# A later turn for attention's products, more steps in the gated layer, and other places for first-used tiles

## The chip, the cores and the metric

The kernel runs on one core of a Trainium2 chip. The metric is the device time of one launch in microseconds. Engines are named as in the profile: PE (matrix products), PEld (its weight loads), DVE, ACT, POOL (GpSimd) and SP, which here issues transfers. A line number such as L1310 is a line of the kernel before, also in the listing below.

## What is computed

Four residual blocks follow each other, each wrapped as x + layernorm(f(layernorm(x))): attention, a mixture of eight experts, attention with a distance bias, and a two-layer stack of local attention and gated feed-forward. x is 2 x 1024 x 128, f32. The change bears on the last block, and on its preparation, which runs during the third. One layer of the last block, cut to what matters:

```python
h = shift_token(x)                       # second half of the features from the token before
q, k, v = split(h @ wqkv, 3)             # 8 heads of 64
q = l2norm(q) * qs; k = l2norm(k) * ksc
q, k = rotary_xpos(q, k)
o = local_attention(q, k, v)             # windows of 64 that see themselves and the window before
x = x + o @ wo
h = layernorm(shift_token(x)) * lg + lb
a, g = split(h @ w1 + b1, 2)
x = x + (a * gelu(g)) @ w2 + b2
```

The stack has two such layers (l = 0, 1). Products are made to f32 accuracy: many are three products of high and low 16-bit parts (`mm3`, lines L49, L50, L51).

## The kernel before

The kernel has four phases. Phases 1 to 3 are the first three blocks. During phase 3, phase 4's preparation (constants, tables, normalization of the first half of x by L92, and the transposes of that into a product's layout by L231) is a generator, which is advanced by one `yield` at a time between pieces of phase 3's work.

Phase 4, the last stage, goes over 32 tiles of 128 tokens: layer l = i // 16, batch b = i // 8 % 2, tile t = i % 8. Each tile passes through small stages: `a` (q and k products and the first rotation products), `a1` and `a2` (norms and rotation), `b0` and `cast` (scaling, high 16-bit parts), `b1` (low parts L1236 and L1237, and three DMA transposes through SP that give K, Q and Qz), `v` (V projection, copied by ACT at L1256, and a shifted copy Vs by DMA), `kc`, `c` (score maxima: products L1277 and L1282, reduction into mz L1291), `c2` (transposes mz, L1296, and ACT copies it to mT, L1298), `d` (transposed scores, with the maxima subtracted by a product with mT at L1310; exponential p at L1316), `e` (attention times V L1327, reciprocal L1336, scaled u L1337), `e1` (transpose of the result L1344, copy oT L1346), and `f` (product with wo L1355, added to F at L1356).

A list, `plan`, names the stages with a lateness. In iteration i it calls each stage in list order for tile i minus its lateness, so up to six tiles are in work. The instructions of all calls are chained in that order on each engine (`in_order`): the plan sets the order of every queue, DMA queues included, and no scheduler moves anything across it.

The gated layer (`stage_g`) handles a group of tiles at once: four, and two for each of the last two groups. ENDS lists the tiles that close a group. It is a generator: at each `gated` entry of the plan, every open group is advanced to its next `yield`. Its steps: token shift by products with `sh` (SH: L1368 to L1371) into hc by POOL (L1372) and ACT (L1373); statistics (DVE L81 to L84, POOL L88); the factor nb (L97) and the normalization on ACT (L99); transposes of hc (L1384), gh and hg on ACT (L1388, L1389), their difference gl on DVE (L1391); nine products and gelu (L1398, each set between two loads of ACT's function table); nine more products; the gating (L1409); the product py (L1413) and yT on ACT (L1415); transposes (L1420) and the addition to F (L1422). In layer 1 the final normalization (L92), the residual (L1429) and the output transfer follow.

`aside` holds slower side work: `normalize(1)`, the second half's normalization, from iteration 1, and layer 1's weights from iteration 6. PSUM banks come in rings, with one name for the products of most stages (b).

K, V and Vs are rings of 5, 6 and 6 buffers. They are allocated in ascending order in memory that phase 3 partly still holds; V's extra column of constants is filled by six memsets at L1156, at the stage's start.

Of the kernel before, what the change touches and what calls it, by code (L numbers as in the profile page):

```python
# [10 lines left out]
F32 = mybir.dt.float32  # L11
F32R = mybir.dt.float32r
F16 = mybir.dt.float16
BF16 = mybir.dt.bfloat16
I32 = mybir.dt.int32
AF = mybir.ActivationFunctionType
ALU = mybir.AluOpType
# [226 lines left out]
def phase1(k, X):  # L244
# [9 lines left out]
    with ExitStack() as es:  # L254
# [61 lines left out]
        def values_of(pair, c):  # L316

            b, a = pair // 4, pair % 4
            xTh, xTl = S["x", b]
            vh, vl = V[pair % 2]  # L320
            ps = big().rearrange("p a (t n) -> p (a t) n", t=2)
# [684 lines left out]
def phase4(k, X):  # L1006
# [5 lines left out]
    nc, A = k.nc, k.A  # L1012
    H, HD, HID = 8, 64, 341
    WS = 256.0
    with ExitStack() as es:
# [7 lines left out]
        nc.gpsimd.dma_start(mask0, A["c_mask0"])  # L1023
        identb = cp.tile([128, 128], BF16, name="identb")
        nc.gpsimd.tensor_copy(identb, k.ident)

        pick = cp.tile([128, H, 128], F16, name="pick")
        nc.gpsimd.tensor_copy(pick, k.ident16[:, :H].unsqueeze(2).to_broadcast([128, H, 128]))
# [1 line left out]
        away = cp.tile([128, 128], F16, name="away")  # L1030
        nc.gpsimd.dma_start(away, A["c_away"])
        nc.gpsimd.tensor_tensor(pick, pick, away.unsqueeze(1).to_broadcast([128, H, 128]), ALU.add)
        fac = cp.tile([128, NT], F32, name="fac")
        nc.sync.dma_start(fac, A["c_fac"])

        sh = cp.tile([128, 2, 128], F32, name="sh")
        nc.sync.dma_start(sh, A["c_shift"])
        Z = [cp.tile([128, 4, 256], F16, name=f"Z{i}") for i in range(2)]
# [2 lines left out]
        for m in mTs:  # L1041
            nc.gpsimd.dma_start(m, A["c_rows4"][int(m is mTs[2])])
        for i in range(2):
            nc.gpsimd.memset(Z[i], 0.0)
            nc.gpsimd.memset(mz[i], 0.0)
        F = [cp.tile([128, NT, D], F32, name="F0")]

        def normalize(b):
            x = [X[:, NT * b + t, :] for t in range(NT)]
            dst = [F[b][:, t, :] for t in range(NT)]  # L1050
            if b:
                yield from k.ln_steps(cp, dst, lambda t: x[t])
                return
            mv, rstd = k.ln_stats(cp, lambda t: x[t])
            yield
            k.ln_to(cp, dst, lambda t: x[t], mv, rstd)
# [54 lines left out]
        def stage_x(l, b, c):  # L1111

            hTh = cp.tile([128, 512], F16, name="hTh", bufs=2)
            hTl = cp.tile([128, 512], F16, name="hTl", bufs=2)
            ps = k.transposed(ps_sm, F[b], c)
            k.split_r(hTh[0:64, :], hTl[0:64, :], ps[0:64, :])
# [21 lines left out]
        wp = pool("p4w", 1)  # L1138
        F.append(wp.tile([128, NT, D], F32, name="F1"))
        sp = pool("p4s", 2)  # L1140
# [3 lines left out]
        def bank(kind=None):  # L1144
            turn[0] = (turn[0] + 1) % 7
            return ps[turn[0] // 3].tile([128, 512], F32, name="b1")

        QB = 3
        RV = 6
        RK = 5  # L1150
        K = [wp.tile([128, H, 192], F16, name=f"K{i}") for i in range(RK)]
        V = [wp.tile([128, H, HD + 1], F32, name=f"V{i}") for i in range(RV)]
        Vs = [wp.tile([128, H, HD + 1], F32, name=f"Vs{i}") for i in range(RV)]
        xm = [wp.tile([128, 64], F32, name=f"xm{b}") for b in range(B)]
        for i in range(RV):
            nc.gpsimd.memset(V[i][:, :, HD : HD + 1], WS)  # L1156

        heads = lambda ap: ap.rearrange("p (h d) -> p h d", d=HD)
        where = lambda i: (i // 16, i // 8 % 2, i % 8)
# [68 lines left out]
        def stage_b1(i):  # L1228
# [5 lines left out]
            if t == 0:  # L1234
                nc.gpsimd.memset(K[k0][:, :, 0:64], 0.0)
            nc.gpsimd.tensor_tensor(mid4(k16), pair4(kk), ends(k16), ALU.subtract)  # L1236
# [4 lines left out]
            nc.sync.dma_start_transpose(Qz, fl(Z[i % 2]))  # L1241
            nc.sync.dma_start_transpose(K[k0][:, :, 64:192], fl(k16))
            nc.sync.dma_start_transpose(Q, fl(q16))
            S["q", i] = Q, Qz

        def stage_v(i):
            l, b, t = where(i)
            wvh, wvl = W[l][8:10]
            hTh, hTl = S["h", l, b, t // 4]
            ts = slice(128 * (t % 4), 128 * (t % 4) + 128)  # L1250
            v0, v1 = i % RV, (i + 1) % RV
            if t == 0:
                nc.gpsimd.memset(Vs[v0][0:64, :, :], 0.0)
            pv = bank("b")
            k.mm3(pv, hTh[:, ts], hTl[:, ts], wvh, wvl)
            nc.scalar.copy(V[v0][:, :, 0:HD], heads(pv))  # L1256
            nc.sync.dma_start(Vs[v0][64:128, :, :], V[v0][0:64, :, :])
            if t < NT - 1:
                nc.sync.dma_start(Vs[v1][0:64, :, :], V[v0][64:128, :, :])

        def stage_kc(i):

            t = where(i)[2]
            if t < NT - 1:
                dst = K[(i + 1) % RK][:, :, 0:64]
                nc.scalar.activation(dst, K[i % RK][:, :, 128:192], AF.Copy, scale=fac[:, t : t + 1])

# [33 lines left out]
        def stage_d(i):  # L1301
            l, b, t = where(i)
            k0 = i % RK
            mT, (Q, Qz) = S.pop(("m", i)), S.pop(("q", i))
            p = sp.tile([128, H, 2, 64], F32, name="p")
            for g in range(2):
                st = bank("d").rearrange("p (h w n) -> p h w n", h=4, w=2)
                for j in range(4):
                    h = 4 * g + j
                    nc.tensor.matmul(st[:, j, :, :], pick[:, 4 * (h % 2) + h // 2, :], mT, start=True, stop=False)  # L1310
                    for w in range(2):
                        kw = K[k0][:, h, 64 * w : 64 * w + 128]
                        s = slice(64 * w, 64 * w + 64)
                        nc.tensor.matmul(st[:, j, w, :], kw, Q[:, h, s], start=False, stop=False)
                        nc.tensor.matmul(st[:, j, w, :], kw, Qz[:, h, s], start=False, stop=w == 1)
                nc.scalar.activation(p[:, 4 * g : 4 * g + 4], st, AF.Exp)  # L1316
            S["p", i] = p
# [31 lines left out]
        def stage_f(i):  # L1349
# [4 lines left out]
            for a in range(4):  # L1354
                nc.tensor.matmul(ps, oT[:, a, :], wo[:, a, :], start=a == 0, stop=a == 3)  # L1355
            nc.vector.tensor_tensor(F[b][:, t, :], ps, F[b][:, t, :], ALU.add)  # L1356

        def stage_g(l, b, t0, T):

            w1h, w1l, w2, col = W[l][3:7]  # L1360
            x = F[b]
            g = slice(t0, t0 + T)
            n = 128 * T
            tiles = lambda ap: ap[:, :n].rearrange("p (t d) -> p t d", d=D)
            hc = tiles(sp.tile([128, 512], F32, name="hc"))
# [10 lines left out]
            yield  # L1376
            mv, rstd = k.ln_stats(sp, lambda t: hc[:, t, :], T)
            yield
            k.ln_scalar(sp, [hc[:, t, :] for t in range(T)], mv, rstd)
            yield  # L1380
            yield
            ps = bank()
            for t in range(T):
                nc.tensor.transpose(ps[:, 128 * t : 128 * t + 128], hc[:, t, :], k.ident)  # L1384
            hg = sp.tile([128, 512], F32, name="hg")[:, :n]
            gh = sp.tile([128, 512], F16, name="gh")[:, :n]
            gl = sp.tile([128, 512], F16, name="gl")[:, :n]
            nc.scalar.activation(gh, ps[:, :n], AF.Identity, scale=col[:, 7:8], bias=col[:, 8:9])  # L1388
            nc.scalar.activation(hg, ps[:, :n], AF.Identity, scale=col[:, 7:8], bias=col[:, 8:9])  # L1389
            yield  # L1390
            nc.vector.tensor_tensor(gl, hg, gh, ALU.subtract)  # L1391
            yield
            ges = []
            for i in range(3):
                pg = bank("g")[:, :n]
# [15 lines left out]
            py = bank()[:, :n]  # L1411
            for i in range(3):
                nc.tensor.matmul(py, w2[:, i, :], ges[i], start=i == 0, stop=i == 2)  # L1413
            yT = sp.tile([128, 512], F32, name="yT")[:, :n]
            nc.scalar.activation(yT, py, AF.Identity, bias=col[:, 6:7], scale=1 / WS)  # L1415
            yield
            yield
            ps = tiles(bank())
            for i in range(T):
# [3 lines left out]
            if l == 1:  # L1423
                mv, rstd = k.ln_stats(sp, lambda t: x[:, t0 + t, :], T)
# [8 lines left out]
        ENDS = [3, 7, 11, 15, 19, 23, 27, 29, 31]  # L1433
        gated, aside = [], []

        def advance(gens):
            gens[:] = [g for g in gens if k.in_order(next, g, 0) is None]


        plan = [  # L1440
            (stage_b0, 1), (stage_v, 2), (stage_a, 0), (stage_c2, 3), (gated, 0), (stage_d, 3), (stage_e1, 4),
            (stage_a1, 0), (stage_cast, 1), (stage_f, 5), (gated, 0), (stage_x, 0), (stage_c, 2), (stage_b1, 1),
            (stage_kc, 2), (aside, 0), (gated, 0), (stage_a2, 0), (gated, 0), (stage_e, 3), (aside, 0),
        ]
        i = 0
        while i < 32 + 5 or gated:
            if i == 1:
                aside.append(normalize(1))
                own = es.enter_context(k.pool("p4v", 1, "right"))
                late_weights = weights(1, own, lambda shape: own.tile(shape, F32, name=f"w{shape[1]}"))  # L1450
                k.in_order(next, late_weights)
            if i == 6:
                aside.append(late_weights)
            for f, late in plan:
                n = i - late
                if isinstance(f, list):
                    advance(f)
                elif f is stage_x:
                    if i - 5 in ENDS:
                        l, b, t = where(i - 5)  # L1460
                        T = i - 5 - ([-1] + ENDS)[ENDS.index(i - 5)]
                        gated.append(stage_g(l, b, t - T + 1, T))
                    if i % 4 == 3 and i + 1 < 32:
                        l, b, t = where(i + 1)
                        k.in_order(stage_x, l, b, t // 4)
                elif 0 <= n < 32:
                    k.in_order(f, n)
            i += 1


# [178 lines left out]
```

## Time and profile before

| | us |
|---|---|
| median of 3 runs | 1412.56 (1412.06 to 1414.65) |
| the profiled execution | 1407.81 |
| its span | 1406.0 |
| mT copies (L1298) in iterations 8, 24, 28, 32 (tiles 5, 21, 25, 29) start at | 1082.9, 1262.3, 1305.4, 1351.6 |

| engine | busy us | share of the span |
|---|---|---|
| PE | 1166.7 | 83% |
| DVE | 1050.4 | 75% |
| ACT | 968.2 | 69% |
| POOL | 879.4 | 63% |

The page divides the span into 40 slices of 35.15 us and gives busy tenths:

```profile
PE   4889999999889787757998986688657988988786
DVE  6776666776672798979888789873577778878875
ACT  2877777887665584532898785578567777787674
POOL 1666766786656545642776659575688776757541
```

The last stage begins at about slice 29 and holds the last eleven slices. A row of the timeline has a start, a length, the engine, the line, the operation with its output and inputs, and how many equal instructions were joined; in brackets is the idle time ahead of it and what ended it. The rows of one tile's passage from its maxima to its exponential are a sample:

```profile
1261.06 0.22 PE L1296 MATMUL sm<-ident,mz 128*128 128x128 f16 x1
1262.26 0.24 ACT L1298 COPY mT<-sm 8x128 f16<-8x128 f16 x1
1262.55 0.22 PE L1310 MATMUL b<-mT,pick 128*128 128x128 f16 x1 [1.27 <-ACT mT L1298]
1263.43 1.29 ACT L1316 ACTIVATE p<-b 128x512 f32<-128x512 f32 x2 [0.94 <-PE b L1315]
```

### The profile page before, as it was taken

What the parts mean: (1) busy time and instruction counts of PE and PEld (TensorE: products, weight loads), DVE (VectorE), ACT (ScalarE), POOL (GpSimd) and SP (SyncE); (2) the same over time, 40 slices, a digit from 0 to 9 for tenths busy, and PEclk for the clock granted to TensorE, in tenths of its full rate; (3) what the DMA queues carried; (4) which work ended last, traced back from release to release, by engine and by line L of the source; (5) the groups of instructions that cost most, each with busy time, mean ns of one, the idle gap of its engine ahead of it and who ended that gap; (6) DMA issues with size and microseconds to landing.
All of it is one profiled execution on the core that took longest, in us unless ns stands there. A gap on an engine that the chain in (4) does not pass through costs nothing. (4 is left out here: it accounts for less than half of the span.)

```text
span 1406.0 us, 28397 instructions
## 1 busy us (share of the span) xinstructions
PE 1166.7 (83%) x11534; PEld 728.4 (52%) x11534; DVE 1050.4 (75%) x1965; ACT 968.2 (69%) x1494; POOL 879.4 (63%) x632
## 2 busy tenths in 40 slices
PE   4889999999889787757998986688657988988786
PEld 1456666666556565444454453343335555655554
DVE  6776666776672798979888789873577778878875
ACT  2877777887665584532898785578567777787674
POOL 1666766786656545642776659575688776757541
PEclk8999999999999898888999998898779999999999
DMA  2000000010000302200000020000075745654440
GB/s 74 1 2 2 2 2 1 2 32 2 1 2 17 105 15 88 64 6 4 5 5 3 5 68 12 9 12 1 1 146 103 135 88 95 115 91 89 99 95 15
DMA packets 122530, 56.75 MB, mean 40 GB/s; under 512 B 105216, under 2 KB 114320, under 8 KB 122400
## 3 DMA queue, kind: packets, MB, share of 16 engines
q1 hardware_dynamic: 119920, 53.53, 18.1%
q8 instruction: 90, 1.47, 0.4%
q10 hardware_dynamic: 1472, 1.09, 0.3%
q0 software_dynamic: 1008, 0.33, 0.2%
q14 instruction: 40, 0.33, 0.1%
HBM read 20.99 MB, written 1.11 MB: 16 GB/s over the span
## 5 line engine op out<-in xcount | busy, mean ns | idle before, releaser
L377 POOL TENSOR_TENSOR hl<-p,hl 128x1024 f16<-128x1024 f32 x128 | 273.8, 2142 | 138.7 <-ACT hl L376 112.1
L909 POOL TENSOR_TENSOR hl<-pt,hl 128x2048 f16<-128x2048 f32 (+1 forms) x48 | 164.7, 3435 | 108.3 <-ACT hl L908 75.9
L342 DVE TENSOR_REDUCE nm<-big 128x2 f32<-128x1024 f32 x128 | 155.1, 1219 | 32.0 <-PE big L339 31.3
L374 ACT ACTIVATE p<-big 128x1024 f32<-128x1024 f32 x128 | 130.8, 1022 | 52.9 <-PE big L370 52.0
L49 PEld LDWEIGHTS <-hl 128*128 128x128 f16 x1024 | 100.6, 98 | 74.0 <-DVE acc L402 41.6
L376 ACT CAST hl<-p 128x1024 f16<-128x1024 f32 x128 | 133.8, 1045 | 4.1
L875 DVE TENSOR_REDUCE mx<-bankz 128x1 f16<-128x512 f32 (+3 forms) x156 | 99.6, 656 | 27.2 <-PE bankz L870 21.8
L904 ACT ACTIVATE pt<-bank 128x512 f32<-128x512 f32 (+1 forms) x173 | 97.1, 596 | 27.7 <-PE bank L903 12.6
L875 DVE TENSOR_REDUCE mx<-bank 128x1 f16<-128x512 f32 (+1 forms) x148 | 94.1, 655 | 16.8 <-PE bank L866 10.8
L49 PE MATMUL pu<-V1h,hl 128*128 128x129 f16 x512 | 92.6, 224 | 12.4 <-DVE acc L402 11.7
L50 PEld LDWEIGHTS <-hl 128*128 128x128 f16 x1024 | 101.4, 99 | 0.0
L49 PE MATMUL pu<-V0h,hl 128*128 128x129 f16 x512 | 93.3, 225 | 9.1 <-DVE acc L402 7.5
L51 PEld LDWEIGHTS <-hl 128*128 128x128 f16 x1024 | 100.5, 98 | 0.0
L904 ACT ACTIVATE pt<-bankz 128x512 f32<-128x512 f32 (+1 forms) x131 | 74.5, 593 | 32.9 <-PE bankz L903 23.6
L51 PE MATMUL pu<-V0h,hl 128*128 128x129 f16 x512 | 92.7, 223 | 0.0
L50 PE MATMUL pu<-V0l,hl 128*128 128x129 f16 x512 | 92.7, 222 | 0.0
L51 PE MATMUL pu<-V1h,hl 128*128 128x129 f16 x512 | 92.0, 222 | 0.0
L50 PE MATMUL pu<-V1l,hl 128*128 128x129 f16 x512 | 92.0, 221 | 0.0
L908 ACT CAST hl<-pt 128x2048 f16<-128x2048 f32 (+1 forms) x48 | 78.2, 1630 | 12.6 <-PE pu L926 12.3
L1193 POOL TENSOR_TENSOR rot<-rot,t 128x512 f32<-128x512 f32 x64 | 80.2, 1273 | 6.5 <-DVE t L1184 6.3
L88 POOL TENSOR_TENSOR ln_rstd<-ln_rs,nhalf 128x4 f32<-128x4 f32 (+2 forms) x30 | 35.5, 1184 | 74.1 <-DVE ln_rs L84 51.1
L901 PE MATMUL bank<-qst,kz 128*128 128x512 f16 (+3 forms) x222 | 66.5, 344 | 15.8 <-DVE mx L875 10.0
(408 smaller groups left out, 3844.4 us busy)
## 6 DMA issues: line engine op xcount, KB each, us to landing
sb<-sd SPq DMA_DIRECT2D x16, 512.0 KB, 4.3
Vs<-V SPq DMA_DIRECT2D x60, 130.0 KB, 2.6
work<-in_t_w SPq DMA_DIRECT2D x3, 512.0 KB, 3.7
out<-F SPq DMA_DIRECT2D x3, 256.0 KB, 2.3
X<-in_L_attn_x SPq DMA_DIRECT2D x2, 256.0 KB, 3.5
w<-in_t_wqk SPq DMA_DIRECT2D x1, 512.0 KB, 4.8
wv<-in_t_wv ACTq DMA_DIRECT2D x1, 512.0 KB, 4.1
X<-in_L_attn_x ACTq DMA_DIRECT2D x1, 512.0 KB
```

The source lines that it names most:

```text
L49: mm(out, lh, rh, start=start, stop=False, **kw)
L50: mm(out, lh, rl, start=False, stop=False, **kw)
L51: mm(out, ll, rh, start=False, stop=stop, **kw)
L342: S["red"] = nc.vector.tensor_reduce(S["n", u][:, i // 2, c, :], ps, AX.X, ALU.max, negate=True)
L374: S["exp"] = nc.scalar.activation(p, st, AF.Exp, scale=QSCALE**-2)
L376: nc.scalar.copy(hl[:, 0], p)
L377: S["lo"] = nc.gpsimd.tensor_tensor(hl[:, 1], p, hl[:, 0], ALU.subtract)
L875: S["max"] = nc.vector.tensor_reduce(out, ps[:, :, :n], AX.X, ALU.max, negate=True)
L904: S["exp"] = nc.scalar.activation(pt[:, a0 : a0 + m, :w], st[:, :, :w], AF.Exp)
L908: nc.scalar.copy(hl[:, 0, :, :w], pt[:, :, :w])
L909: nc.gpsimd.tensor_tensor(hl[:, 1, :, :w], pt[:, :, :w], hl[:, 0, :, :w], ALU.subtract)
L1193: nc.gpsimd.tensor_tensor(rot[:, j], rot[:, j], t2[:, j], ALU.add)
```

## The change

The plan is ordered anew. `e` has lateness 4 instead of 3 and stands between `c2` and `d`, rather than at the iteration's end. `e1` follows `kc`; `b1` follows `e1`, near the end; `x` (the input transposes) stands before the first gated slot; `kc` comes after `c` and `aside`. The gated slots stand after `x`, after `f`, after `b1` and after `a2`; before, they stood after `c2`, after `f`, after `aside` and after `a2`. A group is opened at the end of an iteration rather than at the place of `x`. `stage_g` has more steps: the factor nb, ACT's normalization, the transposes, gh with hg, py, and yT are each on their own, and groups of four have two more after gl, where groups of two have none.

p gets three buffers; hg and yT get one each. The preparation has five more resting points. K, V and Vs are allocated with the last buffer first, so that buffer 0, used first, gets the highest place. V's constant column is filled in `stage_v` for the first six tiles. `normalize(1)` is put aside in iteration 2 instead of 1.

```diff
@@ preparation of phase 4
         nc.gpsimd.tensor_copy(identb, k.ident)
+        yield
...
         nc.gpsimd.tensor_tensor(pick, pick, away.unsqueeze(1).to_broadcast([128, H, 128]), ALU.add)
+        yield
...
         for i in range(2):
+            yield
             nc.gpsimd.memset(Z[i], 0.0)
             nc.gpsimd.memset(mz[i], 0.0)
+        yield
...
-        K = [wp.tile([128, H, 192], F16, name=f"K{i}") for i in range(RK)]
-        V = [wp.tile([128, H, HD + 1], F32, name=f"V{i}") for i in range(RV)]
-        Vs = [wp.tile([128, H, HD + 1], F32, name=f"Vs{i}") for i in range(RV)]
+        K, V, Vs = [None] * RK, [None] * RV, [None] * RV
+        for i in reversed(range(RV)):
+            if i < RK:
+                K[i] = wp.tile([128, H, 192], F16, name=f"K{i}")
+            V[i] = wp.tile([128, H, HD + 1], F32, name=f"V{i}")
+            Vs[i] = wp.tile([128, H, HD + 1], F32, name=f"Vs{i}")
         xm = [wp.tile([128, 64], F32, name=f"xm{b}") for b in range(B)]
-        for i in range(RV):
-            nc.gpsimd.memset(V[i][:, :, HD : HD + 1], WS)
@@ stage_v
+            if i < RV:
+                nc.gpsimd.memset(V[v0][:, :, HD : HD + 1], WS)
@@ stage_d
-            p = sp.tile([128, H, 2, 64], F32, name="p")
+            p = sp.tile([128, H, 2, 64], F32, name="p", bufs=3)
@@ stage_g
             mv, rstd = k.ln_stats(sp, lambda t: hc[:, t, :], T)
             yield
-            k.ln_scalar(sp, [hc[:, t, :] for t in range(T)], mv, rstd)
+            yield
+            nb = sp.tile([128, T], F32, name="ln_nb")
+            nc.vector.scalar_tensor_tensor(nb, mv[:, :, 0], -1.0, rstd, ALU.mult, ALU.mult)
+            yield
+            for t in range(T):
+                nc.scalar.activation(hc[:, t, :], hc[:, t, :], AF.Identity, scale=rstd[:, t : t + 1], bias=nb[:, t : t + 1])
...
                 nc.tensor.transpose(ps[:, 128 * t : 128 * t + 128], hc[:, t, :], k.ident)
-            hg = sp.tile([128, 512], F32, name="hg")[:, :n]
+            yield
+            hg = sp.tile([128, 512], F32, name="hg", bufs=1)[:, :n]
...
             nc.vector.tensor_tensor(gl, hg, gh, ALU.subtract)
-            yield
+            if T == 4:
+                yield
+                yield
...
                 nc.tensor.matmul(py, w2[:, i, :], ges[i], start=i == 0, stop=i == 2)
-            yT = sp.tile([128, 512], F32, name="yT")[:, :n]
+            yield
+            yT = sp.tile([128, 512], F32, name="yT", bufs=1)[:, :n]
             nc.scalar.activation(yT, py, AF.Identity, bias=col[:, 6:7], scale=1 / WS)
             yield
-            yield
@@ the plan
         plan = [
-            (stage_b0, 1), (stage_v, 2), (stage_a, 0), (stage_c2, 3), (gated, 0), (stage_d, 3), (stage_e1, 4),
-            (stage_a1, 0), (stage_cast, 1), (stage_f, 5), (gated, 0), (stage_x, 0), (stage_c, 2), (stage_b1, 1),
-            (stage_kc, 2), (aside, 0), (gated, 0), (stage_a2, 0), (gated, 0), (stage_e, 3), (aside, 0),
+            (stage_b0, 1), (stage_v, 2), (stage_a, 0), (stage_c2, 3), (stage_e, 4), (stage_d, 3), (stage_a1, 0),
+            (stage_cast, 1), (stage_x, 0), (gated, 0), (stage_f, 5), (gated, 0), (stage_c, 2), (aside, 0), (stage_kc, 2),
+            (stage_e1, 4), (stage_b1, 1), (gated, 0), (stage_a2, 0), (gated, 0), (aside, 0),
         ]
         i = 0
         while i < 32 + 5 or gated:
+            if i == 2:
+                aside.append(normalize(1))
             if i == 1:
-                aside.append(normalize(1))
...
-                    if i - 5 in ENDS:
-                        l, b, t = where(i - 5)
-                        T = i - 5 - ([-1] + ENDS)[ENDS.index(i - 5)]
-                        gated.append(stage_g(l, b, t - T + 1, T))
...
+            if i - 5 in ENDS:
+                l, b, t = where(i - 5)
+                T = i - 5 - ([-1] + ENDS)[ENDS.index(i - 5)]
+                gated.append(stage_g(l, b, t - T + 1, T))
             i += 1
```

## The prediction

> **What bounds the kernel now.** The sum below is made against the profiled execution: 1407.81 us, span 1406.0. The median of the runs shown is 1412.56, so 4.75 above it, and I add 4.75 at the end. I read the page's busy shares first, then the last stage (about 1000 to 1406) cut into stretches, then the waits of each engine there, then single rows.
>
> The first view is busy time in stretches (columns: length, then busy time of PE, PEld, DVE, ACT, POOL, then granted clock, DMA share, GB/s). A cycle of the last stage is four tiles, after which its gated layer repeats.
>
> ```profile
> 880.00:890.00 10.00, 3.90 (x17) 2.34 (x16) 9.69 (x11) 0.58 (x1) 5.47 (x2) 0.50 0.11 28
> 1174.20:1217.70 43.50, 39.61 (x488) 26.68 (x488) 35.15 (x70) 33.49 (x74) 29.18 (x41) 0.96 0.53 96
> 1217.70:1262.30 44.60, 38.48 (x490) 25.34 (x490) 35.80 (x72) 34.10 (x76) 28.56 (x39) 1.00 0.60 96
> ```
>
> In a cycle no engine is full: PE stands 4 to 6 us of 44, DVE 8 to 9, ACT 10. So waits set the cycle. The chain that ended last is shared evenly, which says the same:
>
> ```profile
> PE 8%; ACT 8%; DVE 7%; issue 2%; POOL 2%; DMA 0%; POOLq 0%; DVEq 0%; ACTq 0%
> ```
>
> PE's waits from 1080 to 1345 (six cycles), with ACT's largest after the dots:
>
> ```profile
> PE b L1310 <- ACT mT L1298: 14.1, 12, 2.6
> PE b L1368 <- DVE F L1356: 5.2, 5, 1.6
> PE b L50 <- DVE gl L1391: 4.9, 5, 1.1
> PE b L1384 <- ACT hc L99: 3.7, 4, 1.7
> ...
> ACT hc L99 <- DVE ln_nb L97: 24.9, 6, 5.8
> ACT yT L1415 <- PE b L1413: 9.8, 5, 2.0
> ```
>
> All PE rows there sum to 34.9 us, 5.8 a cycle. The largest is the score products waiting for the transposed maxima mT, once every second tile.
>
> **The change, term by term.** The instruction counts stay the same on every engine: no work is added or removed, only order, buffers and addresses.
>
> *Before the stage (phase 3's end).* Phase 4's preparation now has more resting points, so normalize(0) and the input transposes (L231) come later in the queues. Today DVE is held by that normalization while POOL writes its tables, and PE stands behind it:
>
> ```profile
> 874.35 12.49 DVE L92 TENSOR_SCALAR F<-X,ln_mv,ln_rstd 128x128 f32<-128x128 f32 x8
> ...
> PE sm L231 <- DVE F L92: 8.7, 3, 5.1
> ```
>
> Eight rows at the median 0.34 would be 2.7; they took 12.49, one alone 6.17. In the changed order five more reductions (L875, 0.65 each) stand ahead of them on DVE, and about 5 us of products that phase 3 owes anyway stand ahead of L231 on PE. The gain is what that work covers: -5, between 0 (the next reduction waits instead) and -8.7 (all three waits).
>
> [...]
>
> *The stage's first tile.* K, V and Vs are allocated in reversed order, and the six memsets of V's column leave the stage's start for the first six V projections.
>
> ```profile
> 1023.65 0.29 POOL L1156 MEMSET V<- 128x8 f32 x6 [2.71 <-issue]
> ```
>
> Those memsets stood 2.70 us for memory that phase 3's last rows (X, 1022.85 to 1023.54) give back; K's memset, k's low part, the DMA of K (3.18) and the first maxima follow in the chain. With tile 0 in space freed earlier, K's memset can follow the normalization's rstd (1019.89 + 1.04) directly: -2.8, between 0 (ACT's copy into V stands there too, only 0.77 of it) and -3.
>
> *The loop.* I laid the four iterations out by hand, every queue in its changed order, with durations from rows: e 1.05, d 1.42, f 0.89, e1 0.5, c 0.87, the nine gated products 1.95, py 2.64 on PE; F 0.25, mz 1.25, stats 1.75, the three gates 1.95 on DVE; p 0.5 twice, LN 1.4, gelu 1.85 plus two table loads of 1.28 on ACT; hc 0.81, low k 1.15 on POOL. From mT to mT:
> - first, 8.8: DVE sets it. F, the residual add, a rest until POOL's hc at 5.4, four stats, and mz ends at 8.45.
> - second, 10.8: ACT. e (L1327) now stands between the transposes of the maxima and d (L1310), so its 1.05 covers the mT wait (about 1.2 each); but e1 then waits for u.
> - third, 13.5 or, with the input transposes' casts, 14.3: ACT. It holds gelu, two loads and the casts (2.1 to 2.9).
> - fourth, 11.2: PE, with pas, f, c, e1, py, v, a.
>
> That is 44.7 a cycle with the third at its mean of about 13.9, against 43.7 as the mean of the undisturbed cycles before (first rows of V at 1081.44, 1125.56, 1172.82, 1216.21, 1260.81, 1303.98). So the removed mT wait is given back: ACT between mT and p stands 0.94 in an iteration where no gated step fills it, and the changed plan has none there in any iteration. From mT in iteration 8 to mT in iteration 32 (tiles 5 and 29) before took 268.7 (1082.9 to 1351.58). After, by the same layout: iteration 8, 7.2; the first cycle, whose gated work is thinner, 44.1; four cycles 178.8; iterations 29 to 31, which make no input transposes, 34.4; the late normalization and weights 1.4. Sum 265.9, so -2.8. Bounds: -14 (the mT rows vanish and nothing takes their place) and +8.5 (ACT's 0.94 in three of four tiles, 2.8 a cycle, half of it bare over six cycles). I take -2.8, since the hand layout uses rows and most of its error is common to both kernels. Of the moved steps b1 also issues three DMA transposes on SP (about 1.3 each, 3.2 to landing); they now leave behind e1, and c needs them one iteration later, some 6 us off, so I cost them at nothing; without that cover they cost up to 3.2 a tile. The buffers go with the order: p lives one tile longer and gets a third; hg and yT drop to one each, and are asked for again only with the next group, four tiles (over 40 us) later. V's column is set once per buffer, six rows that total 0.29, on a POOL that is busy 28.6 of 44.6. All three at nothing, 0.29 in all if POOL were full.
>
> *The tail.* The last group now starts one iteration's slots later and has more steps, so other groups' work precedes it.
>
> ```profile
> 1388.35 0.27 ACT L1373 COPY hc<-b 128x128 f32<-128x128 f32 x1 [0.64 <-PE b L1371]
> ...
> 1402.04 0.60 DVE L92 TENSOR_SCALAR F<-F,ln_mv,ln_rstd 128x128 f32<-128x128 f32 x2 [0.90 <-POOL ln_rstd L88]
> ```
>
> Before, f of the last tile is at 1385.8 and hc at 1388.35, 2.6 later. After, PE does py(27) 2.64, two transposes 0.4, four transposes 0.66 and group 29's products 0.98 first (4.7), and ACT that group's gelu 0.83 and the load behind it: hc 9.5 after f, +6.9. From hc to the end 18.55 by my layout against 17.65: +0.9. f itself comes 32.9 after mT of iteration 32, against 34.2: -1.3. Sum +6.5, between +3 (only PE's part less f's 1.3) and +9 (the whole 9.5).
>
> **Sum:** -5 - 2.8 - 2.8 + 6.5 = -4.1; 1403.7 profiled, 1408.5 as a median.
>
> **The rivals.**
> - *ACT takes the loop's wait.* Place: between mT and p, where LN, gelu and yT used to stand and now nothing does. For it: ACT's third iteration is full by my layout, and yT and LN rows fall elsewhere. Against: ACT has 10 us a cycle free. Price +8.5 in place of -2.8: -5 - 2.8 + 8.5 + 6.5 = +7.2, 1419.8. It decides the sign once the loop loses more than 1.3 us, which is 0.2 a cycle.
> - *PE's waits really go.* The mT row (14.1) disappears and the hc, gl and F rows do not grow. For it: PE is the fullest engine and the four rows shown are 27.9 of its 34.9. Against: the second and third iteration are bound by ACT. -5 - 2.8 - 14 + 6.5 = -15.3, 1397.3.
> - *The change does not do what it says ahead of the loop.* POOL still waits for phase 3's last rows and PE waits under another name for the same normalization. For it: K's memset follows the rstd that itself waited 5.32 for DVE. -2.8 + 6.5 = +3.7, 1416.3.
>
> **Chances.** The forecast 0.47, its own range 1402 to 1415; ACT 0.25; PE's waits gone 0.18; nothing ahead of the loop 0.10. About 0.2% (2.8 us) is what a measurement of this kernel can tell from no change. The forecast gives 0.27 faster, 0.13 same, 0.07 slower; ACT 0.02, 0.04, 0.19; waits gone 0.18 faster; the last 0.01, 0.03, 0.06: 0.48, 0.20, 0.32. The range 1393 to 1424 takes in the second rival with 4 us below it and the first with 4 above.
>
> **What would show it.** Right: no wait of L231 over 2 us before 900; K's memset directly after rstd near 1021; the L1310 row on mT far below 14.1, and larger ACT waits at p; mT 44 to 45 apart in fours; hc of the last group some 9 us after its f. Wrong: mT in fours over 46 or under 43, a wait on the DMA of K in c, or an end less than 56 or more than 64 us after mT of iteration 32.

## The result and the profile after

The changed kernel took 1432.27 us (median of 4 runs, 1431.91 to 1435.12) against 1412.32 of the kernel before in the same session: a ratio of 1.0142, 95% interval 1.0124 to 1.016. It is slower by 20 us; the prediction said 1408.5. Its profiled execution took 1432.09, with a span of 1430.3 against 1406.0, so 24.3 longer. The starts of the mT copies divide that (L1298 before; the lines of the changed kernel are numbered 5 to 15 higher in the last stage, and here it is L1305):

| stretch, by mT of iterations | before | after | difference |
|---|---|---|---|
| start to 8 | 1082.9 | 1078.9 | -4.0 |
| 8 to 12 | 44.1 | 50.1 | +6.0 |
| 12 to 16 | 47.3 | 48.7 | +1.4 |
| 16 to 20 | 43.4 | 44.8 | +1.4 |
| 20 to 24 | 44.6 | 47.3 | +2.7 |
| 24 to 28 | 43.2 | 45.5 | +2.3 |
| 28 to 32 | 46.2 | 45.4 | -0.8 |
| 32 to the end | 54.4 | 69.6 | +15.2 |

The front gained; the loop lost 13, the tail 15. The waits of the loop are of another kind than before. These are PE's and DVE's largest in the changed kernel from 1078 to 1320 (engine, line, what it waited for: total us, times, longest).

```profile
PE b L50 <- DVE gl L1404: 14.0, 5, 3.1
PE b L1317 <- ACT mT L1305: 12.2, 9, 2.2
PE b L1289 <- DMA K<-k: 8.5, 5, 3.4
PE sm L1303 <- DVE mz L1298: 4.2, 5, 1.5
...
DVE rot L1186 <- ACT acc L1184: 46.5, 16, 5.3
```

In the kernel before, the row of gl came to 4.2 in the same stretch, and two of these rows did not occur at all: PE's wait for the transposed K, and DVE's 46.5 us for acc, the squares that ACT makes at an iteration's start. Why acc is late is seen on ACT. First one passage of the kernel before, then the same work in the changed kernel (timeline, ACT).

```profile
1282.70 1.09 ACT L1179 ACTIVATE acc<-b 128x512 f32<-128x512 f32 x2
1283.66 0.24 ACT L1298 COPY mT<-sm 8x128 f16<-8x128 f16 x1
1283.92 1.28 ACT L1398 ACT_TABLE_LOAD   x1
1285.21 1.84 ACT L1398 ACTIVATE ge<-b,col 128x512 f32<-128x512 f32 x3
1287.08 1.28 ACT L73 ACT_TABLE_LOAD   x1
1288.37 1.08 ACT L1316 ACTIVATE p<-b 128x512 f32<-128x512 f32 x2
```

```profile
1263.36 1.28 ACT L1413 ACT_TABLE_LOAD   x1
1264.65 1.84 ACT L1413 ACTIVATE ge<-b,col 128x512 f32<-128x512 f32 x3
1266.52 1.28 ACT L73 ACT_TABLE_LOAD   x1
1267.81 0.22 ACT L1207 ACTIVATE rz<-ss 128x16 f32<-128x16 f32 x1
...
1268.43 0.57 ACT L1263 COPY V<-b 128x512 f32<-128x512 f32 x1
1268.89 1.09 ACT L1184 ACTIVATE acc<-b 128x512 f32<-128x512 f32 x2
1269.86 0.24 ACT L1305 COPY mT<-sm 8x128 f16<-8x128 f16 x1
```

The same 4.4 us of gelu and its loads stood behind mT in the kernel before, with p next in the queue, which is not needed until e at the iteration's end; now they are ahead of rz, V, acc and mT, and three engines wait for those. POOL and DVE in the same moment of the changed kernel:

```profile
1268.66 0.22 POOL L1210 TENSOR_TENSOR rz<-rz,ss 128x16 f32<-128x16 f32 x1 [7.58 <-ACT rz L1209]
...
1269.52 0.69 DVE L1186 TENSOR_TENSOR rot<-b,tab 128x512 f32<-128x512 f32 x1 [4.52 <-ACT acc L1184]
```

At the front the counterparts of the lines shown of before are these, of DVE, PE and POOL. The first row is a tiny maximum that ran while POOL wrote tables:

```profile
864.50 10.02 DVE L880 TENSOR_TENSOR mx<-mx,mx 128x16 f16<-128x16 f16 x1
877.18 0.48 PE L866 MATMUL bank<-kz,qst 128*128 128x384 f16 x1 [9.98 <-DVE mx L875]
888.16 3.63 DVE L92 TENSOR_SCALAR F<-X,ln_mv,ln_rstd 128x128 f32<-128x128 f32 x8
1018.81 1.04 POOL L88 TENSOR_TENSOR ln_rstd<-ln_rs,nhalf 128x4 f32<-128x4 f32 x1 [6.95 <-DVE ln_rs L84]
1019.80 0.53 POOL L1240 MEMSET K<- 128x512 f16 x1
```

The eight normalizations now take 3.63 instead of 12.49, but a maximum ahead of them takes 10.02, and PE waits 9.98 for DVE where it had waited 5.08 at most. So phase 3 gained little: the rstd row that closes it comes at 1018.81 instead of 1019.89. K's memset does follow it directly: 1019.80 against 1023.86, of which 3.0 is the placement.

The tail (PE and ACT of the changed kernel):

```profile
1404.48 0.39 PE L1375 MATMUL b<-F,sh 128*128 128x128 f32 x2
1406.92 0.27 ACT L1380 COPY hc<-b 128x128 f32<-128x128 f32 x1
1410.68 2.90 PE L1428 MATMUL b<-ge,w 128*128 128x256 f32 x6 [4.44 <-DVE ge L1424]
1420.41 2.34 PE L1428 MATMUL b<-ge,w 128*128 128x256 f32 x6
```

The last group's hc is 10.4 behind the start of its f (1396.52), against 2.7 before (f at 1385.66), and from there to the end it takes 23.4 against 17.65.

### The profile page after: what moved, and what is told of

It is laid out like the page before. It is cut to its first block, busy times and chain, and to the rows that moved or that the text cites. A ratio compares the mean times of both kernels' runs of the same rounds, so it can differ in the third digit from the quotient of the medians.

```text
span 1430.3 us, 28374 instructions
## 1 busy us (share of the span) xinstructions
PE 1173.5 (82%) x11534; PEld 736.4 (51%) x11534; DVE 1041.1 (73%) x1965; ACT 973.1 (68%) x1494; POOL 882.2 (62%) x632
## 4 chain that ended last, share of the span: by engine, by line
PE 41%; DVE 31%; ACT 14%; POOL 7%; issue 6%; DMA 1%; SPq 0%; POOLq 0%; ACTq 0%; DVEq 0%
DVE mx L875 6%; PE big L370 4%; PE pu L49 4%; PE pu L51 3%; PE pu L50 3%; DVE nm L342 3%; PE pu L926 3%; ACT pt L904 2%; PE b L1428 2%; DVE hl L652 2%; POOL rot L1220 1%; PE bank L901 1%; POOL rot L1198 1%; PE big L49 1%; PE big L51 1%
## 5 line engine op out<-in xcount | busy, mean ns | idle before, releaser
L904 ACT ACTIVATE pt<-bank 128x512 f32<-128x512 f32 (+1 forms) x173 | 97.1, 601 | 32.2 <-PE bank L903 14.4
L49 PE MATMUL pu<-V1h,hl 128*128 128x129 f16 x512 | 92.6, 224 | 12.4 <-DVE acc L402 11.7
L1198 POOL TENSOR_TENSOR rot<-rot,t 128x512 f32<-128x512 f32 x64 | 80.3, 1275 | 10.4 <-DVE t L1189 10.3
L1186 DVE TENSOR_TENSOR rot<-b,tab 128x512 f32<-128x512 f32 x64 | 43.7, 683 | 56.0 <-ACT acc L1184 54.7
```

What stands on the lines that cost most here:

```text
L49: mm(out, lh, rh, start=start, stop=False, **kw)
L904: S["exp"] = nc.scalar.activation(pt[:, a0 : a0 + m, :w], st[:, :, :w], AF.Exp)
L1198: nc.gpsimd.tensor_tensor(rot[:, j], rot[:, j], t2[:, j], ALU.add)
```

## The experiments

Each session ran the kernel before beside the others, and its median was 1408.9 to 1409.4 there; ratios are to that kernel, with 95% intervals, and differences between experiments go by these ratios. Line numbers in a view are those of the kernel it shows. The plan's lists are the edits. Experiments 1 to 4 took the change apart by my first theory.

**1. The front alone**, in the kernel before: the five `yield`s, the reversed allocation, the column in `stage_v`.

> The kernel before with the front of the change alone: five more resting points in the preparation, K, V and Vs from the last buffer down, V's column filled in stage_v. Theory: the front is a gain that the rest of the change eats. In the changed kernel POOL's low k starts at 1020.29 against 1024.34, so this kernel should gain about 4 us, 1408 to 1409, of which some 3 from the placement (no 2.71 of issue ahead of K's memset) and 1 from phase 3. Rival: what is won there is lost at the next wait in the loop, 1411 to 1413.

Ratio 0.9973 (0.9963 to 0.9983), -3.8 us, with 268.7 from mT of iteration 8 to 32, as before. As expected; the front is a gain and the rest of the change costs some 24. A single profile would not have told it: with this same front the first mT came between 1028.2 and 1035.0 in the profiled executions of different kernels.

**2. The aside slot back**

```diff
-            (stage_cast, 1), (stage_x, 0), (gated, 0), (stage_f, 5), (gated, 0), (stage_c, 2), (aside, 0), (stage_kc, 2),
-            (stage_e1, 4), (stage_b1, 1), (gated, 0), (stage_a2, 0), (gated, 0), (aside, 0),
+            (stage_cast, 1), (stage_x, 0), (gated, 0), (stage_f, 5), (gated, 0), (stage_c, 2), (stage_kc, 2),
+            (stage_e1, 4), (stage_b1, 1), (aside, 0), (gated, 0), (stage_a2, 0), (gated, 0), (aside, 0),
```

> The changed kernel with the first aside slot put back behind kc, e1 and b1. Theory: the 20.14 us between mT of iterations 11 and 12 come from layer 1's table product (L1104), which in the changed plan stands on POOL ahead of b1's low k and waits 5.17 for a transfer; with the slot behind b1 that gap falls to about 13 and the time by 6 to 8 us, to 1424 to 1426. Rival: the hole belongs to the K transposes issued too late; then the gap stays above 17 and the time above 1429.

Ratio 1.0144 (1.012 to 1.0168), the same as the changed kernel. The gap between iterations 11 and 12 fell only from 20.1 to 17.75, and 8 to 12 from 50.1 to 48.7. So the table product's wait is the smaller part of that stretch. These are the rival's numbers, but its cause is not shown either: experiment 8 issues the transposes early and gains as little.

**3. The former steps of the gated layer in the changed plan**

```diff
-            yield
-            nb = sp.tile([128, T], F32, name="ln_nb")
-            nc.vector.scalar_tensor_tensor(nb, mv[:, :, 0], -1.0, rstd, ALU.mult, ALU.mult)
-            yield
-            for t in range(T):
-                nc.scalar.activation(hc[:, t, :], hc[:, t, :], AF.Identity, scale=rstd[:, t : t + 1], bias=nb[:, t : t + 1])
+            k.ln_scalar(sp, [hc[:, t, :] for t in range(T)], mv, rstd)
...
-            yield
             hg = sp.tile([128, 512], F32, name="hg", bufs=1)[:, :n]
...
-            if T == 4:
-                yield
-                yield
+            yield
...
-            yield
             yT = sp.tile([128, 512], F32, name="yT", bufs=1)[:, :n]
             nc.scalar.activation(yT, py, AF.Identity, bias=col[:, 6:7], scale=1 / WS)
+            yield
             yield
```

> The changed kernel with the gated layer's former steps (one buffer each for hg and yT kept), plan unchanged. Theory: the additional steps cost twice, in the loop because gelu falls into the iteration with the input transposes (PE waits for gl 2.5 to 3.1 a cycle, mT 2.0 to 2.2), and at the end because the last groups' work comes an iteration later; without them about 1.5 us a cycle and 6 to 9 us at the end go, 1417 to 1421. Rival: the plan's order itself (e between c2 and d) sets the loop and the late f; then 1428 or more.

Ratio 1.0232 (1.0212 to 1.0252): 13 us slower than the change, not faster. The loop went to 48.3 to 54.2 a cycle, and PE's wait for mT to 37.2 us. Only at the end did the theory hold: from mT of iteration 32 to the end 59.8 instead of 69.6. In the loop, the added steps are a remedy for something else in the plan: with the former steps ACT stands 21.5 us in 5 for nb and 13.3 in 4 for py (from 1078 to 1320), where the changed kernel has no wait for nb and 5.5 in 4 for py.

**4. x behind the first gated slot**

```diff
-            (stage_cast, 1), (stage_x, 0), (gated, 0), (stage_f, 5), (gated, 0), (stage_c, 2), (aside, 0), (stage_kc, 2),
+            (stage_cast, 1), (gated, 0), (stage_x, 0), (stage_f, 5), (gated, 0), (stage_c, 2), (aside, 0), (stage_kc, 2),
```

> The changed kernel with the input transposes behind the first gated slot, so that gl no longer stands behind hTl on DVE. Theory: the row PE L50 <- gl falls from 14.0 (5) to below 4, but ACT's gelu and two table loads still stand ahead of V, acc and mT, so only 1 to 1.5 of the 2.8 a cycle are won: 1425 to 1428. Rival: gl is the cause by itself and the cycle falls by the whole 2.8: 1418 to 1421.

Ratio 1.0214 (1.0194 to 1.0234). The row of gl fell to 0.3 as meant, and PE's wait for mT rose to 22.7: taking away the largest wait of PE made it slower. The waiting for gl was a symptom.

So all of my first theory fell but the front and the tail. Experiments 5 to 8 ask which part of the plan it is.

**5. The third gated slot to between e and d**, groups opened at f:

```diff
-            (stage_b0, 1), (stage_v, 2), (stage_a, 0), (stage_c2, 3), (stage_e, 4), (stage_d, 3), (stage_a1, 0),
+            (stage_b0, 1), (stage_v, 2), (stage_a, 0), (stage_c2, 3), (stage_e, 4), (gated, 0), (stage_d, 3), (stage_a1, 0),
...
-            (stage_e1, 4), (stage_b1, 1), (gated, 0), (stage_a2, 0), (gated, 0), (aside, 0),
+            (stage_e1, 4), (stage_b1, 1), (stage_a2, 0), (gated, 0), (aside, 0),
```

> The changed kernel with the third gated slot moved from behind b1 to between e and d, where the kernel before had one, and groups opened at f, so that the nine products with gelu and py fall into that slot. Theory A: the changed plan lost the place where ACT's gated work lay in the shadow of mT's way to PE and back; gelu and its table loads now stand at the iteration's end, ahead of the next tile's rz, V, acc and mT. Then the cycle of four falls from 45 to 48 to about 44, and the time to within 5 us of the kernel before. Theory B: e between c2 and d, or b1 at the end, sets the cycle; then it stays over 45.5 and the time 12 us or more above before.

Ratio 1.0187 (1.0157 to 1.0216): B by the numbers. Gelu did go back behind mT, and DVE's row of acc fell from 46.5 to 11.1, but the loop grew from 281.8 to 289.5. So that row alone does not set the changed loop. The edit also shifted every other step, and PE's largest wait became one for F ahead of gated products (10.8 in 5); how much of A is left cannot be read from it.

**6. Only e later**, on experiment 1 (p with three buffers, hg and yT with one):

```diff
-            (stage_b0, 1), (stage_v, 2), (stage_a, 0), (stage_c2, 3), (gated, 0), (stage_d, 3), (stage_e1, 4),
+            (stage_b0, 1), (stage_v, 2), (stage_a, 0), (stage_c2, 3), (stage_e, 4), (gated, 0), (stage_d, 3),
...
-            (stage_kc, 2), (aside, 0), (gated, 0), (stage_a2, 0), (gated, 0), (stage_e, 3), (aside, 0),
+            (stage_kc, 2), (stage_e1, 4), (aside, 0), (gated, 0), (stage_a2, 0), (gated, 0), (aside, 0),
```

> The kernel of e1_front with attention's products alone moved: e with lateness 4 between c2 and the gated slot ahead of d, e1 behind kc, three buffers for p, one for hg and yT; gated slots, steps, x and b1 as before. Theory A: the move by itself costs little, cycle 43 to 44.5, time within 4 us of before (the gain of the front partly given back). Theory B: e ahead of d lengthens the way from mT to p and oT by 0.5 to 1 a tile, 13 us or more above e1_front.

Ratio 1.0007 (0.9992 to 1.0021): A: within 4 us of the kernel before, but some 5 us above experiment 1. PE's mT wait fell from 12.8 to 7.9, and other waits took the place.

**7. Only the gated part**: slots, opening and steps as changed, attention's order as before.

```diff
-            (stage_b0, 1), (stage_v, 2), (stage_a, 0), (stage_c2, 3), (stage_e, 4), (stage_d, 3), (stage_a1, 0),
-            (stage_cast, 1), (stage_x, 0), (gated, 0), (stage_f, 5), (gated, 0), (stage_c, 2), (aside, 0), (stage_kc, 2),
-            (stage_e1, 4), (stage_b1, 1), (gated, 0), (stage_a2, 0), (gated, 0), (aside, 0),
+            (stage_b0, 1), (stage_v, 2), (stage_a, 0), (stage_c2, 3), (stage_d, 3), (stage_e1, 4), (stage_a1, 0),
+            (stage_cast, 1), (stage_x, 0), (gated, 0), (stage_f, 5), (gated, 0), (stage_c, 2), (stage_b1, 1),
+            (stage_kc, 2), (aside, 0), (gated, 0), (stage_a2, 0), (gated, 0), (stage_e, 3), (aside, 0),
```

> The changed kernel with attention's order put back (e last with lateness 3, e1 behind d, b1 and kc behind c, ahead of aside), while the gated slots, the opening of groups and the steps stay as changed. Theory A: slow as the changed kernel, cycle above 45, end some 10 us longer behind mT of iteration 32, so 12 to 20 us above before. Theory B: near before in the loop, 43 to 44 a cycle, and only the end longer, 4 to 8 us above before.

Ratio 1.0236 (1.0207 to 1.0264): slow, some way beyond A, with 47.3 to 51.5 a cycle. The cost is in the gated part; attention's move wins back 13 us of it.

**8. b1 back behind c**

```diff
-            (stage_cast, 1), (stage_x, 0), (gated, 0), (stage_f, 5), (gated, 0), (stage_c, 2), (aside, 0), (stage_kc, 2),
-            (stage_e1, 4), (stage_b1, 1), (gated, 0), (stage_a2, 0), (gated, 0), (aside, 0),
+            (stage_cast, 1), (stage_x, 0), (gated, 0), (stage_f, 5), (gated, 0), (stage_c, 2), (stage_b1, 1), (aside, 0),
+            (stage_kc, 2), (stage_e1, 4), (gated, 0), (stage_a2, 0), (gated, 0), (aside, 0),
```

> The changed kernel with b1 alone put back directly behind c. Theory A: the waits of c for the K transpose (8.5 us in 5) go, but most of it returns as waits for mT; 2 to 5 us are won, 15 to 18 above before. Theory B: the late transposes are what sets the loop; 8 us or more are won, less than 12 above before.

Ratio 1.0135 (1.0101 to 1.017), not to be told from the change, whose interval it overlaps; PE's wait for K's transfer fell only from 8.5 to 6.6. An earlier b1 gains next to nothing here, so its late place is not what the change lost.

Experiments 9 and 10 test the place of one slot by itself, in the kernel of experiment 1.

**9. The slot between c2 and d to ahead of v**

```diff
-            (stage_b0, 1), (stage_v, 2), (stage_a, 0), (stage_c2, 3), (gated, 0), (stage_d, 3), (stage_e1, 4),
+            (stage_b0, 1), (gated, 0), (stage_v, 2), (stage_a, 0), (stage_c2, 3), (stage_d, 3), (stage_e1, 4),
```

> The kernel of e1_front with one word moved: its first gated slot stands ahead of v instead of between c2 and d. Steps, opening, attention's order are as in e1_front. Theory C: the place of this slot is what the changed kernel lost. ACT's normalization (with its wait for nb, 4.6 at the longest), gelu with two loads and yT then stand ahead of V, acc and mT, on which DVE's rotation and PE's scores wait, instead of behind mT, where only p follows, which nobody needs before the iteration's end. Then the cycle rises by 3 to 4 us, to 46.5 to 48, and the time to 15 to 25 us above e1_front. Theory D: the place does not matter and the steps or the opening of groups do; within 4 us of e1_front.

Ratio 1.035 (1.0313 to 1.0387), 53 us above experiment 1, more than twice what was expected: 50.0 to 55.8 a cycle. The row that the changed kernel had brought appears in the kernel before, from this one move (DVE, then PE, 1078 to 1320):

```profile
DVE rot L1186 <- ACT acc L1184: 41.7, 13, 4.4
...
PE b L1317 <- ACT mT L1305: 47.9, 18, 7.9
```

and the timeline of ACT has the same picture as the changed kernel's, with nothing else of the change but the front:

```profile
1263.90 1.28 ACT L1405 ACT_TABLE_LOAD   x1
1265.20 1.84 ACT L1405 ACTIVATE ge<-b,col 128x512 f32<-128x512 f32 x3
1267.06 1.28 ACT L73 ACT_TABLE_LOAD   x1
1268.35 0.58 ACT L1263 COPY V<-b 128x512 f32<-128x512 f32 x1
1268.83 1.09 ACT L1184 ACTIVATE acc<-b 128x512 f32<-128x512 f32 x2
1269.80 0.24 ACT L1305 COPY mT<-sm 8x128 f16<-8x128 f16 x1
```

Gelu is only part of the 53. From iteration 24 to 28 the four steps from mT to mT take 14.3, 14.4, 12.4 and 9.4, against 10.2, 11.4, 10.6 and 11.1 in experiment 1. The first now holds the normalization, the second gelu, the third yT. With the former steps ACT waits in the first and the third, and the wait stands ahead of V:

```profile
1303.46 1.65 ACT L99 ACTIVATE hc<-hc,ln_nb,ln_rstd 128x128 f32<-128x128 f32 x4 [4.33 <-DVE ln_nb L97]
1330.71 0.69 ACT L1422 ACTIVATE yT<-b,col 128x512 f32<-128x512 f32 x1 [4.21 <-PE b L1420]
```

The step with gelu is 3.0 longer, that with the normalization 4.1. In the changed kernel, whose added steps take the wait for nb away, the cycle from 24 to 28 is only 2.3 longer than before, and its longest step is again the one with gelu (14.3).

**10. The control: that slot behind d**

```diff
-            (stage_b0, 1), (stage_v, 2), (stage_a, 0), (stage_c2, 3), (gated, 0), (stage_d, 3), (stage_e1, 4),
+            (stage_b0, 1), (stage_v, 2), (stage_a, 0), (stage_c2, 3), (stage_d, 3), (gated, 0), (stage_e1, 4),
```

> The control for e9: the same slot behind d instead of ahead of it, so ACT's gated work follows p and still stands behind mT. Theory C: 3 us or less from e1_front, to either side. Theory D': only the shadow between mT and p's products hides the gated work; then the cycle rises by 1.5 or more and the time by 8 or more.

Ratio 1.0024 (1.001 to 1.0039), 7 us above experiment 1, between the two expectations: 44.5 to 44.7 in the undisturbed cycles instead of 43.2 to 43.4. PE's wait for mT doubled (25.2 in 21, against 12.8 in 11), since its gated products no longer fill it. So the place has two effects in this kernel: PE's shadow of mT, worth 7 us in all, and ACT's gated work, with the waits in it, ahead of V, acc and mT, worth most of the 53.

**11. Attention's part of the change whole**: the changed plan with the gated layer's former steps, slots between e and d and behind f, b1 and a2, groups opened ahead of c, and `normalize(1)` put aside in iteration 1.

```diff
+            (stage_b0, 1), (stage_v, 2), (stage_a, 0), (stage_c2, 3), (stage_e, 4), (gated, 0), (stage_d, 3), (stage_a1, 0),
+            (stage_cast, 1), (stage_x, 0), (stage_f, 5), (gated, 0), (stage_c, 2), (aside, 0), (stage_kc, 2),
+            (stage_e1, 4), (stage_b1, 1), (gated, 0), (stage_a2, 0), (gated, 0), (aside, 0),
```

> The attention part of the change whole (e, e1, b1, kc, x and aside in the changed order, front, buffers), with the gated layer as before: its four slots between e and d, behind f, behind b1, behind a2, its former steps, groups opened ahead of c. Theory C: within 5 us of e6 and so of the kernel before, 1405 to 1414 on this footing. Theory D: the late b1 and the early x cost by themselves; 10 us or more above before.

Ratio 0.9985 (0.9972 to 0.9999), as theory C has it: under 2 us from experiment 1, so e, the late b1 and the early x together cost nothing that counts. Experiment 3 has the same order of attention and the same former steps, and differs from this kernel only in the slots, the opening of groups and one iteration in `normalize(1)`: 1.0232, so these are worth 2.5%, some 35 us.

**12 and 13. More steps, slots unmoved.** In experiment 1, nb and the normalization apart, the second in the slot behind f, which stood empty; then also py and yT apart.

```diff
-            k.ln_scalar(sp, [hc[:, t, :] for t in range(T)], mv, rstd)
+            nb = sp.tile([128, T], F32, name="ln_nb")
+            nc.vector.scalar_tensor_tensor(nb, mv[:, :, 0], -1.0, rstd, ALU.mult, ALU.mult)
             yield
+            for t in range(T):
+                nc.scalar.activation(hc[:, t, :], hc[:, t, :], AF.Identity, scale=rstd[:, t : t + 1], bias=nb[:, t : t + 1])
             yield
```

> The kernel of e1_front with the gated layer's factor nb and ACT's normalization on two steps, the second in the slot behind f that stood empty. ACT no longer waits for nb (23.6 us in 6) ahead of p. Theory C: that wait lay where it cost little, so 2 us or less are won. Rival: it was on the path; 5 us or more faster than e1_front.

Ratio 0.9908 (0.9881 to 0.9934), 1397.84 us: the fastest of all, 9 us ahead of experiment 1 where 2 were expected. So ACT's wait for nb (23.6 us in 6), which stood ahead of p, did lie on the path. The gain is mostly in the disturbed cycles (12 to 16, 44.8 against 47.3; 20 to 24, 42.5 against 44.6).

> e12_front_ln with py and yT on two steps as well, yT in the empty slot behind f; all slots as in the kernel before. Theory C: more steps are no loss in themselves, so this kernel stays faster than before; ACT's wait for py (9.8 us in 5) goes from ahead of p, 0 to 5 us faster than e12. Theory D: more steps cost; 5 us or more slower than e12.

Ratio 0.9949 (0.9935 to 0.9963), 1400.10: faster than before, but slower than experiment 12, by 2 us in the medians and 6 by the ratios, whose intervals do not meet. Both splits together are a gain, the second by itself is not.

**14. The whole change but for the slots' places**: experiment 11 with both splits.

> e11_attention_only with the same two splits (nb from the normalization, py from yT): the whole change but for the place of the slots and the opening of groups. Theory C: 5 us or more faster than before, since the steps are an improvement where the slots stay put. Theory D: no faster than e11; the steps gain only with the former order of attention.

Ratio 0.9939 (0.9922 to 0.9957), 1399.67. Against 1.0142 for the change, the place of the slots, the opening at the iteration's end, the few other steps and `normalize(1)` one iteration later are worth 2%, some 28 us. None of these four was tested by itself in this plan.

Put together, with the front in each (ratio to before):

| | former steps | more steps |
|---|---|---|
| former slots, former attention | 0.9973 | 0.9908, 0.9949 |
| former slots, e later | 1.0007, 0.9985 | 0.9939 |
| changed slots, former attention | not run | 1.0236 |
| changed slots, e later | 1.0232 | 1.0142 (the change) |

In the upper rows the added steps gain, and the later e costs 5 us at most; in the lower ones each wins back some 13 us of what the slots lose.

## Why the prediction was wrong

**The loop's sum** is the step that failed: -2.8 forecast, +13.1 measured. Put beside the prediction's own terms, by the starts of mT:

| iterations | before | forecast | after |
|---|---|---|---|
| 8 to 9 | 9.8 | 7.2 | 8.3 |
| 9 to 13, "the first cycle" | 46.3 | 44.1 | 53.2 |
| 13 to 29, "four cycles" | 178.9 | 178.8 | 186.0 |
| 29 to 32 | 33.8 | 34.4 | 34.3 |
| late normalization and weights | | 1.4 | in the rows above |

The layout of an undisturbed cycle was good, and not by luck: between iterations 16 and 20 the four steps took 11.1, 8.5, 11.3 and 14.0, where it has 11.2 (its fourth), 8.8, 10.8 and 13.9. But I used that cycle for all four, and only two of them ran like it (44.8 and 45.5); the others took 48.7 and 47.3, and their counterparts before (47.3 and 44.6) were long as well. The forecast "four cycles" thus equals a stretch of before that holds such disturbances, and 1.4 was all I gave the changed kernel for them. My own rise of 1.0 a cycle (44.7 against 43.7), put on the measured loop of before, would have been about +6 in place of -2.8, and the sum -5 - 2.8 + 6 + 6.5 = +4.7: slower.

**The mechanism** was nearest to the rival "ACT takes the loop's wait", whose time, 1419.8, was too low. The engine was right, the place wrong. I looked for the loss "between mT and p", in the hole that nothing fills now. Experiment 10 prices that hole at 7 us, in the kernel of experiment 1. The larger part is on the other side: where the removed slot's work went, to ahead of V, acc and mT (experiment 9). The layout had ACT set the third iteration at 13.9 with gelu in it (14.3 measured between iterations 27 and 28), and so had the price of gelu's new place in an undisturbed cycle. That the slots, with the opening of groups and `normalize(1)`, cost the changed plan some 35 us with the former steps is shown by experiments 3 and 11; which of the queue's waits carries it there is argued from the traces, and experiment 5 speaks against acc alone.

**PE's wait for mT** did not go "far below 14.1": from 1078 to 1320 it is 14.1 in 12 before and 12.2 in 9 after. That e's 1.05 covers it holds better with the slots left alone: 12.8 in experiment 1 falls to 7.9 in experiment 6, 4.3 in 11 and 1.0 in 14.

**The DMA transposes**, costed at nothing, do show a wait of c (8.5 in 5), against my "some 6 us off"; no experiment shows it on the path.

**The front**: -7.8 forecast, -4.0 measured, -3.8 in experiment 1. The placement was right (2.8 forecast, 3.0 measured). The phase 3 term was -5 and came to -1.1: the wait took another name, as its lower bound had it. With the eight rows moved away L880 took 10.02 while POOL worked, for 128x16 elements whose median is 1.0; in the kernel before it took 4.58 there.

**The tail**: +6.5 forecast (3 to 9), +15.2 measured. The term "hc 9.5 after f, +6.9" was near: 10.4, +7.7. "From hc to the end +0.9" was mis-sized: +5.7. DVE does group 27's final normalization and group 29's gates (1408.31 to 1411.23) ahead of the last group's nb, PE stands 4.44, and its granted clock falls from 1.00 to 0.50; I had taken py's duration from the tail before, where it was 1.00 (1389 to 1400). f itself came 1.7 later behind mT of iteration 32 (35.8 against 34.1) instead of 1.3 earlier. Experiment 3 puts 9.8 of the 15.2 on the added steps.

What stays open: the +6.0 between iterations 8 and 12, where layer 1's weights arrive. One step grew by more than that, 20.1 between 11 and 12 against 11.1 before. There POOL's table product waits 5.17 for a transfer, rot comes behind it on POOL, and ACT waits for rot:

```profile
1115.79 0.62 ACT L1228 CAST k<-rot 128x512 f16<-128x512 f32 x1 [4.19 <-POOL rot L1220]
```

Experiments 2 and 8 took 1.4 and 1.3 of the +6.0 away, and with the slots in their old places the stretch is 45.3 (experiment 14) against 50.1, with a wait of 5.14 in the same place. Which wait sets it in the changed kernel was not found. `normalize(1)` one iteration later stands in every kernel over 1.01 but experiment 9 and was not tested alone.

## What to carry to other kernels

In these queues, which run in the plan's order, a step's price was set by what stood behind it: one slot cost 53 us ahead of v and 7 behind d, both against experiment 1. Gelu with its loads is the same 4.4 us on ACT in both kernels; ahead of values that three engines need, in experiment 9, the step with it was 3.0 longer, and a normalization that itself had to wait 4.1. So when a step is moved, list for each queue the next three instructions behind its new place and who waits for them.

The largest wait in a table need not be the one to remove: experiment 4 removed PE's and lost 10 us more. And when a hand layout is set against a measured stretch, both must hold the same disturbances.

## What the runs showed of the hardware

In the changed kernel POOL worked without a pause from 863.93 to 874.4 (a scaling, a subtraction of phase 3 and three table products), and one DVE instruction of 128x16 f16 elements, L880, took 10.02 us in that stretch; eight of that kind had a median of 1.02 and a minimum of 0.21. In the kernel before it took 4.58 there, and eight rows of 128x128 behind it 12.49. So it was not the size of the DVE instruction that set how long it took; what did, no run shows.

The granted clock at the tail was 1.00 from 1390 to 1406, 0.75 from 1406 to 1411 and 0.50 from 1411 to 1415 (the windows of the changed kernel), where PE stood 4.44 us; the same six products of py took 2.90 and 2.34 there, and 1.53 and 1.56 in the kernel before, at 1.00.

```profile
1406.00:1411.00 5.00, 0.56 (x4) 0.35 (x2) 3.65 (x14) 1.18 (x2) 1.70 (x2) 0.75 0.00 0
1411.00:1415.00 4.00, 3.44 (x10) 2.35 (x10) 0.51 (x3) 1.35 (x3) 0.00 (x0) 0.50 0.22 66
1389.33 1.53 PE L1413 MATMUL b<-ge,w 128*128 128x256 f32 x6 [1.02 <-DVE ge L1409]
```

In windows of 1 us the clock is 1.00 until 1408, 0.76 from 1408 to 1409 and 0.50 from there to 1422, so by my estimate (0.76 as a mean of 1.00 and 0.50) it fell about 2.3 us after PE's last product had ended (1406.24). Beside the 4.44 us of PE's wait, the products of py took 2.2 us longer than in the kernel before. That the wait brought the lower clock is my reading of the order in time; no run tests it.
